# A graph layer on one core: chunks of 896 edges for 768, 58 steps for 68, pieces dealt behind the next sums, another last order, four loads under way for five

## The chip, the core and the metric

The kernel runs on one core of a Trainium2 chip. The metric is device time in microseconds (us) of one execution; lower is better. The core has TensorE (PE; its weight loads are listed as PEld), VectorE (DVE), ScalarE (ACT), GpSimd (POOL) and SyncE (SP, which here only issues DMAs), and 16 DMA engines. SBUF has 128 partitions, PSUM holds what PE writes.

## What is computed

One layer of a graph network, all in float32: 12500 nodes with 128 features, 412500 edges with 48 features, sorted by their target node `dst`. The features of a node's edges are summed; the node's own features are normalised; both go through two dense layers, with a residual.

```python
h = jnp.maximum(_layernorm(x, axis=-1), 0.0)
# in the layer: nodes = h, edges = edge_attr_48
agg = jax.ops.segment_sum(edges, recv, num_segments=N_NODES)   # recv = dst
u = graph_globals[batch]                                       # batch is all 0
z = jnp.concatenate([nodes, agg, u], axis=1)                   # 128 + 48 + 64
h2 = jax.nn.relu(z @ W1 + b1)                                  # 256
x = x + (h2 @ W2 + b2)
```

## The kernel before

**Edges.** The edges are cut into chunks of `CE = 768`: `T = 6` consecutive edges in each of 128 partitions, so that a partition's row is 6 x 48 x 4 = 1152 bytes. There are 537 chunks and 84 edges over. Since the edges are sorted, the targets of one chunk lie within a window of `W = 32` consecutive nodes. Eight chunks (`CS`) make a step, four (`CH`) a half step; 67 whole steps and a last one of one chunk and the rest make `NS = 68`.

For a step, `load` (L259) has SP issue four DMAs of two chunks each. `onehot` (L265) has DVE compare the edges' positions in their windows (`rel`) with 0 to 31; the result is a 128 x 32 matrix of zeros and ones for each of the 48 groups of edges. `aggregate` (L287) has PE multiply them with the edges' features: four chunks use four column groups of 32, and the products of a half step lie side by side in one PSUM bank. `keep_sums` (L301) has ACT copy the sums to SBUF. `place_columns` (L308, DVE) makes a matrix of zeros and ones that says at which node of the step each of the 128 sums belongs, `place` (L314) multiplies with it on PE, and `add` (L323, DVE) adds the outcome, 218 columns wide, into `aggT`, the sums of all nodes, at a column that is read from the data (`at_i`, within 47 of a planned centre, `SLACK`).

**Targets.** `dst` comes in five parts of up to 128 chunks. `load_dst` loads a part with a chunk in each partition, `shift_dst` (L178) subtracts a reference, the chunk's middle edge less 16, `spread_dst` (L229) transposes it on PE into `rel`, in two halves of three edge positions, `own_and_ref` (L190) and `middles` (L201) work out where chunks and steps belong. `check_dst`, `deviation`, `worst_of_all` and `verdict` find whether a target lies outside its window; if one does, a general branch behind `tc.If` (L744) computes everything again.

**Nodes.** 12500 nodes make 26 blocks: one of 212, 23 of 512, and two of 256 at the end, `x1` and `x2`. A block goes through `load_x`, `stats`, `root`, `factors`, `plus_b2`, `normal` (normalisation), `turn` and `keep` (transposed and copied), `first_h` (the x part of the first layer), `first_a` (the part of the sums, once its steps are added), `relu`, `second` (second layer, two rows of 128 nodes a call), `result` and `store`. Stores go by POOL's queue, those of the last two blocks by SP's.

**Order.** Each engine does its instructions in the order in which the program writes them. The loop over steps (L694) writes: placement of an earlier step, loads of the step `AHEAD - 1 = 4` further on, what is dealt to half step `2s`, the add, what is dealt to `2s + 1`, the step's sums, copies, comparisons for two steps further on. From `LATE = NS - 8` on a step is placed one step after its sums instead of two. `piece` (L601) deals PE's pieces of the layers (turn, first_h, first_a, second) to half steps, one after another, by a cost in us and a room per half step: `SHARE = 1.05`, and 1.3 for the last 28 half steps. Loads and normalisation of a block are dealt at fixed distances ahead of its turn (`load_x` 20 half steps, L638).

**Loads under way.** `few` (L254) makes each load of edges (and the later ones of x and dst) wait until the load `FLIGHT = 5` before it has landed. There are 22 buffers for edges (L140), each of two chunks.

**The end** is written by hand (L722 to L738): first layer of x2 (its x part), x1's sum part and relu, placement and add of the last step, x1's second layer, result and store, then the same for x2.

Of the kernel before, what the change touches and what calls it, by code (L numbers as in the profile page):

```python
# [22 lines left out]
def kernel(  # L23
# [25 lines left out]
    T = 6  # L49
# [5 lines left out]
    BEFORE, SECOND, WP = 118, 102, 116  # L55
# [5 lines left out]
    assert NCH == NSF * CS + 1 and TAIL % T == 0 and 0 < TAIL  # L61
    TP = TAIL // T


    PER = 11
# [3 lines left out]
    HALF = (2 * CH + 1) * CE * N // (2 * E)  # L69
    LAST = (2 * NCH - 1) * CE * N // (2 * E)  # L70
    SLACK = 47

    def centre(s):
        return SPAN * (s // PER) + EACH * (s % PER) + HALF if s < NSF else LAST

# [52 lines left out]
    def load_tail(e):  # L128
        nc.sync.dma_start(e[:TP], edge_attr[NCH * CE:E].rearrange("(p t) d -> p (t d)", t=T))

# [8 lines left out]
    with fast:  # L139
        ep = fast.enter_context(tc.tile_pool(name="edges", bufs=22))  # L140
# [11 lines left out]
        NCK = 4 * len(parts) + 2  # L152
# [25 lines left out]
        def shift_dst(i):  # L178
            c0, rows = parts[i]
            di = dsts[i]  # L180
            sub = dp.tile([P, 1], F32, name="sub")
            mid = dp.tile([P, 1], F32, name="mid")
# [4 lines left out]
            dsts[i] = df, mid  # L187


        def own_and_ref(i):  # L190
            n, rows = parts[i][1] // CS, parts[i][1]
            df, mid = dsts[i]
            a = dp.tile([P, P // CH], F32, name="own")
            nc.vector.tensor_scalar(a[:rows, :2 * n], same_h[:rows, :2 * n], mid[:rows], None, OP.mult)
            b = dp.tile([P, P // CS, 2], F32, name="ref")
            nc.vector.tensor_scalar(
                b[:rows, :n], perm[:rows, 0].rearrange("k (s h) -> k s h", h=2)[:, :n, 1:2].to_broadcast([rows, n, 2]),
                mid[:rows], -1.0, OP.mult, OP.mult)
            dsts[i] = df, mid, a, b

        def middles(i):  # L201
# [3 lines left out]
            _, mid, a, b = dsts[i]  # L205
            pt = ps_t.tile([P, 512], F32, name="pt") if i else ps_o.tile([P, 512], F32, name="po")
            nc.tensor.matmul(pt[:, :2 * n], same_c[:rows].rearrange("k c w -> k (c w)"), a[:rows, :2 * n],
# [4 lines left out]
            nc.tensor.matmul(pt[0:1, row:row + n], mid[:rows],  # L212
                             perm[:rows, 0].rearrange("k (s h) -> k s h", h=2)[:, :n, 1], start=False, stop=True,
                             skip_group_check=True)
            m = n
            if i == len(parts) - 1:
                nc.tensor.matmul(pt[0:1, row + n:row + n + 1], mid[:rows], perm[:rows, 0, 2 * n:2 * n + 1],
                                 start=False, stop=True, skip_group_check=True)
                m = n + 1
            nc.vector.tensor_tensor(pos[:, s0:s0 + n], pt[:, :2 * n].rearrange("p (s h) -> p s h", h=2),  # L220
                                    wcol[:, None, :].to_broadcast([P, n, 2]), OP.add)
            r = slice(s0, s0 + m)
            mf = dp.tile([1, P], F32, name="mf")
            nc.vector.tensor_tensor(dev[:, r], pt[0:1, row:row + m], cen[:, r], OP.subtract)
# [4 lines left out]
        def spread_dst(i, h):  # L229
            c0, rows = parts[i]  # L230
            dv = dsts[i][0].rearrange("c (p t) -> c t p", t=T)
            pool, name = ((ps_o, "po"), (ps_h, "ph"))[i] if h and i < 2 else (ps_t, "pt")
            pt = pool.tile([P, 512], F32, name=name)
            for t in range(3):
                nc.tensor.transpose(pt[:, t * rows:(t + 1) * rows], dv[:rows, 3 * h + t, :], ident[:rows, :rows])
            nc.scalar.copy(
                rel[:, c0:c0 + rows, 3 * h:3 * h + 3].rearrange("p c t -> p t c"),
                pt[:, :3 * rows].rearrange("p (t c) -> p t c", t=3))

        def outside(v, n, m, col, most=over):  # L240
            sc = mp.tile([P, CE], F32, name="sc")
# [17 lines left out]
        def load(s, h):  # L259
            for c in range(CH * h, CH * (h + 1), 2) if s < NSF else range(2 * h, 2, 2):  # L260
                e = ep.tile([P, 2, T * DE], F32, name="e")
                few(load_edges(e, s * CS + c, 2 if s < NSF else 1))
                edges.setdefault(s, []).extend([e[:, 0], e[:, 1] if s < NSF else etail])

        def onehot(s):  # L265
# [10 lines left out]
            if s == NSF:  # L276
                chunks(0, 1)
                compare(P, T, 2 * T, relt)
# [7 lines left out]

        def aggregate(s, h):  # L287
            whole = s < NSF
            if h == 0:
                banks_s[s] = ps_agg.tile([P, 512], F32, name="ps")[:, :2 * DE].rearrange("p (h f) -> p h f", h=2)  # L290
                if not whole:
                    return
            ps, es, oh = banks_s[s], edges[s], onehots[s]
            for t in range(T):
                for q in range(CH) if whole else range(2):
                    c = CH * h + q if whole else q
                    nc.tensor.matmul(  # L297
                        ps[W * q:W * (q + 1), h], oh[:, c * T + t], es[c][:, t * DE:(t + 1) * DE],
                        start=(t == 0 and (h == 0 or not whole)), stop=(t == T - 1), skip_group_check=True)

        def keep_sums(s):  # L301
            h = slice(0, 2) if s < NSF else slice(1, 2)
            k = P if s < NSF else 2 * W
            to = sums[s % NSB].rearrange("p h (u f) -> p h u f", u=2)[:k, h, :, :DE]
            ps = banks_s.pop(s)
            nc.scalar.copy(to, ps[:k, h, None, :].to_broadcast([k, h.stop - h.start, 2, DE]))  # L306
# [7 lines left out]
        def place(s):  # L314
            banks_p[s] = pp = ps_p.tile([P, 512], F32, name="pp")
            po = places.pop(s)
            whole = s < NSF
            k = P if whole else 2 * W
            for h in range(2) if whole else (1,):
                nc.tensor.matmul(pp[:HI + DE, SECOND * h:SECOND * h + WP], sums[s % NSB][:k, h, :HI + DE], po[:k, h],  # L320
                                 start=(h == 0 or not whole), stop=(h == 1), skip_group_check=True)

        def add(s):  # L323
# [3 lines left out]
            a = 0 if s < NSF else SECOND  # L327
            to = aggT[:, ds(v[0] + a, WG - a)]
            nc.vector.tensor_tensor(to, to, banks_p.pop(s)[:HI + DE, a:WG], OP.add)  # L329
# [68 lines left out]
        def bank(j, h):  # L398
            n = blocks[j][1] * blocks[j][2]
            small = bank_is_shared(j)  # L400
            if h == 0 or not small:
                pool, name = (ps_t, "pt") if j == NBL - 2 else (ps_h, "ph")
# [77 lines left out]
        tail_di = one.tile([P, T], I32)  # L480
# [3 lines left out]
        def load_tail_dst():  # L484
            ta = NCH * CE
            at = ta - CE // 2
            load_tail(etail)
            with nc.allow_non_contiguous_dma(reason="84 numbers, once"):
                nc.sync.dma_start(tail_di[:TP], dst[ta:E].rearrange("(p t) -> p t", t=T))
                nc.sync.dma_start(tail_md[:TP], dst[None, at:at + 1].to_broadcast([TP, 1]))  # L490

        def tail_dst():
            sub = one.tile([P, 1], F32)
            nc.vector.tensor_scalar(sub[:TP], tail_md[:TP], float(-W // 4), None, OP.add)
            nc.vector.tensor_scalar(relt[:TP], tail_di[:TP], sub[:TP], None, OP.subtract)
            outside(relt[:TP], TP, T, 4 * len(parts))
            nc.vector.tensor_copy(pos[:, NSF], wcol[:, 1:2].to_broadcast([P, 2]))
            nc.vector.tensor_scalar(pos[W:2 * W, NSF], pos[W:2 * W, NSF], float(W // 4), None, OP.add)
# [12 lines left out]
        AHEAD = 5  # L511
        EARLY = 2
        FLIGHT = 5
        LATE = NS - 8
        with tc.manual_schedule():
# [14 lines left out]
            nc.gpsimd.memset(cen[:, NSF:NS], float(LAST))  # L530
# [66 lines left out]
            SHARE, LAST_SHARE = 1.05, 1.3  # L597
# [13 lines left out]

            def turned(j):
# [10 lines left out]
            for j in range(NW):  # L623
# [4 lines left out]
                for q in range(0, r, 2):  # L628
# [3 lines left out]
                at(where["o", j] + 1, result, j)  # L632
                at(where["o", j] + 1, store, j)
            where["turn", NBL - 2], where["turn", NBL - 1] = where["turn", NW - 1] + 2, where["turn", NW - 1] + 4
# [32 lines left out]
            for i in range(2, len(parts)):  # L667
                need = 2 * (parts[i][0] // CS)
# [6 lines left out]
                at(k - 16, load_dst, i)  # L675
            at(2 * (NS - 44), clear_tail)
            at(2 * (NS - 40), load_tail_dst)
            at(2 * (NS - 20), tail_dst)
            at(2 * (NS - 10), deviation)
            at(2 * (NS - 9), worst_of_all)  # L680
            apart(2 * (NS - 7), verdict)
# [8 lines left out]
            for h in range(NH):  # L690
                at(where["turn", x2] + 2, first_h, x1, h)
            assert placed(ready[x1]) < NS

            for s in range(NS):  # L694
# [39 lines left out]
            first_a(x2)  # L734
            relu(x2)
# [8 lines left out]
    with tc.If(isbad >= 1):  # L744
# [3 lines left out]
        with tc.tile_pool(name="any", bufs=1) as ap, tc.tile_pool(  # L748
# [37 lines left out]
            for t in range(T):  # L786
                pt = pp.tile([P, P], F32, name="pt2")
                nc.tensor.transpose(pt[:TP, :1], f1.rearrange("c (p t) -> c t p", t=T)[:, t, :], ident[:1, :1])
# [25 lines left out]
            e = ap.tile([P, T * DE], F32, name="e3")  # L814
            load_tail(e)
# [63 lines left out]
```

## Time and profile before

| what | value |
|---|---|
| three runs | median 328.39 us (326.06 to 328.59) |
| the profiled execution | 327.03 us |
| its span, first to last instruction | 325.0 us |
| mean granted TensorE clock | 0.991 |
| DMA | 95.33 MB, mean 293 GB/s |
| comparisons for sums (L269, DVE) | 70 instructions, 117.5 us, 1682 ns each |
| matmuls of the sums (L297, PE) | 6444 records (two for each matmul), 98.2 us |
| placement (L320, PE) | 270 records, 43.8 us, 285 ns each |
| placement columns (L310, DVE) | 68, 38.9 us, 573 ns each |
| add (L329, DVE) | 68, 25.8 us, 379 ns each |
| copy of sums (L306, ACT) | 68, 21.7 us, 318 ns each |

The span is that of the same profiled execution; the 2 us between it and the time lie outside the traced instructions. "Busy" is the time in which an engine has an instruction running; "idle before" is put down to what ended it. A DMA record is one packet (here one row of a partition) on one of the 16 engines. A row of the timeline gives start, length, engine, line, operation, operands, how many were merged, and in brackets the idle time ahead of it with what ended it; SPq is SP's DMA queue.

### The profile page before, as it was taken

The numbers are of one execution on the slowest core, as the hardware profiler recorded it, in microseconds if no ns is written. First come the engines' busy times: TensorE is split into PE (matmuls) and PEld (weight loads), VectorE is DVE, ScalarE is ACT, GpSimd is POOL, SyncE is SP. The second block draws the span as 40 slices with busy tenths as digits, with TensorE's granted clock in tenths as the row PEclk, the third lists the DMA queues.
The fourth block names the chain that finished last, engine by engine and source line by source line (L and its number), as shares of the span: only waits on it lengthen the run. The fifth ranks groups of instructions, "written<-read, shape, count | busy, mean of one in ns | idle before, by whom it ended". The sixth has DMA issues, their size and how long they took to land. (4 is left out here: it accounts for less than half of the span.)

```text
span 325.0 us, 17324 instructions
## 1 busy us (share of the span) xinstructions
PE 281.6 (87%) x7598; PEld 212.8 (65%) x7599; DVE 236.3 (73%) x560; ACT 138.9 (43%) x325; POOL 67.9 (21%) x88
## 2 busy tenths in 40 slices
PE   7789779889879879999788998699998988899992
PEld 3557566767657666778576766476775776676771
DVE  6867978757689757978578867867777789587621
ACT  2226733445346431636183535053654154336410
POOL 8331212033113203201303301204200402301000
PEclk9999999999999998999999999999999999999998
DMA  7999999999999999999989999999999999899611
GB/s 227 281 321 305 302 312 309 308 309 317 314 304 332 295 331 282 316 340 343 337 255 310 310 322 314 290 307 340 310 330 307 285 332 319 275 324 329 212 36 39
DMA packets 80045, 95.33 MB, mean 293 GB/s; under 512 B 5473, under 2 KB 74851, under 8 KB 79964
## 3 DMA queue, kind: packets, MB, share of 16 engines
q1 hardware_dynamic: 77756, 87.53, 85.9%
q0 software_dynamic: 2208, 6.63, 5.3%
q8 instruction: 61, 1.00, 1.4%
q14 instruction: 20, 0.16, 0.2%
HBM read 87.74 MB, written 6.40 MB: 290 GB/s over the span
## 5 line engine op out<-in xcount | busy, mean ns | idle before, releaser
L297 PE MATMUL ps<-e,oh 128*32 128x48 f32 x6444 | 98.2, 208 | 30.8 <-issue 17.3
L297 PEld LDWEIGHTS ps<-e,oh 128*32 128x32 f32 x6444 | 81.5, 110 | 62.6 <-issue 32.2
L269 DVE TENSOR_TENSOR oh<-iota,rel 128x1536 f32<-128x1536 f32 (+1 forms) x70 | 117.5, 1682 | 0.0
L306 ACT COPY sums<-ps 128x192 f32<-128x192 f32 x68 | 21.7, 318 | 129.2 <-PE ps L297 129.2
L329 DVE TENSOR_TENSOR aggT<-aggT,pp 112x218 f32 x68 | 25.8, 379 | 50.0 <-PE pp L320 43.0
L455 POOL DMA_DIRECT2D out_dram<-ot x25 | 13.9, 556 | 230.3 <-DVE ot L447 75.5
L442 PE MATMUL po<-w,hid 128*128 128x128 f32 (+1 forms) x384 | 49.4, 280 | 1.2 <-issue 0.8
L408 PE MATMUL ph<-hT,w1h 128*128 128x512 f32 (+2 forms) x100 | 48.5, 589 | 0.1
L442 PEld LDWEIGHTS po<-w,hid 128*128 128x128 f32 (+1 forms) x384 | 46.4, 195 | 1.9 <-issue 0.9
L320 PE MATMUL pp<-place,sums 128*112 128x116 f32 x270 | 43.8, 285 | 0.7 <-issue 0.7
L433 ACT ACTIVATE hid<-ph,bias 128x512 f32<-128x512 f32 (+2 forms) x49 | 30.4, 670 | 31.8 <-PE ph L422 31.8
L376 ACT ACTIVATE xn<-xt,sh,sc 128x128 f32<-128x128 f32 (+1 forms) x98 | 40.5, 486 | 0.0
L369 POOL TENSOR_TENSOR xb<-xt,b_sb 128x512 f32<-128x512 f32 (+2 forms) x26 | 35.9, 1384 | 15.4 <-DMA xt<-in_x_dram 9.6
L310 DVE TENSOR_TENSOR place<-iota,pos 128x232 f32<-128x232 f32 x68 | 38.9, 573 | 0.0
L320 PEld LDWEIGHTS pp<-place,sums 128*112 128x112 f32 x270 | 32.2, 177 | 5.6 <-issue 1.7
L390 ACT COPY hT<-pt 128x512 f32<-128x512 f32 (+2 forms) x26 | 26.4, 1015 | 7.0 <-PE pt L384 6.9
L422 PE MATMUL ph<-aggT,w1a 48*128 48x256 f32 (+1 forms) x192 | 27.8, 401 | 0.0
L447 DVE TENSOR_TENSOR ot<-po,xb 128x512 f32<-128x512 f32 (+2 forms) x25 | 16.7, 666 | 11.5 <-PE po L442 7.9
L422 PEld LDWEIGHTS ph<-aggT,w1a 48*128 48x128 f32 x192 | 16.8, 186 | 10.5 <-issue 7.1
L346 DVE BATCH_NORM_STATS2 st<-xt 128x6 f32<-128x128 f32 (+1 forms) x98 | 21.3, 279 | 2.9 <-DMA xt<-in_x_dram 2.9
L408 PEld LDWEIGHTS ph<-hT,w1h 128*128 128x128 f32 x100 | 16.4, 194 | 5.9 <-issue 3.1
L384 PE MATMUL pt<-ident,xn 128*128 128x128 f32 (+1 forms) x98 | 17.4, 285 | 1.4 <-ACT xn L376 0.8
(122 smaller groups left out, 143.0 us busy)
## 6 DMA issues: line engine op xcount, KB each, us to landing
e<-in_edge_attr_dram SPq DMA_DIRECT2D x268, 288.0 KB, 4.7
xt<-in_x_dram SPq DMA_DIRECT2D x23, 256.0 KB, 5.0
out_dram<-ot POOLq DMA_DIRECT2D x23, 256.0 KB, 5.0
di<-in_dst_dram SPq DMA_DIRECT2D x3, 384.0 KB, 5.7
di<-in_dst_dram SPq DMA_DIRECT2D x1, 363.0 KB
xt<-in_x_dram SPq DMA_DIRECT2D x2, 128.0 KB, 4.2
out_dram<-ot SPq DMA_DIRECT2D x2, 128.0 KB
e<-in_edge_attr_dram SPq DMA_DIRECT2D x1, 144.0 KB
```

The costliest lines, as they stand in the source:

```text
L269: nc.vector.tensor_tensor(oh[:k, a:b], iota[:k, None, :W].to_broadcast([k, b - a, W]), r[:, :, None].to_broadcast([k, b - a, W]), OP.is_equal)
L297: nc.tensor.matmul(ps[W * q:W * (q + 1), h], oh[:, c * T + t], es[c][:, t * DE:(t + 1) * DE], start=(t == 0 and (h == 0 or not whole)), st ...
L310: nc.vector.tensor_tensor(po, iota[:, None, :WP].to_broadcast([P, 2, WP]), pos[:, s, :, None].to_broadcast([P, 2, WP]), OP.is_equal)
L320: nc.tensor.matmul(pp[:HI + DE, SECOND * h:SECOND * h + WP], sums[s % NSB][:k, h, :HI + DE], po[:k, h], start=(h == 0 or not whole), stop= ...
L329: nc.vector.tensor_tensor(to, to, banks_p.pop(s)[:HI + DE, a:WG], OP.add)
L369: nc.gpsimd.tensor_tensor(xb[:m, :r], xs[j][:m, :r], b2_sb[:m, None, :].to_broadcast([m, r, D]), OP.add)
L376: nc.scalar.activation(xn[:m, q], xs[j][:m, q], AF.Relu, bias=shift[j][:m, q:q + 1], scale=scale[j][:m, q:q + 1])
L390: nc.scalar.copy(hT[:, :m * r].rearrange("d (p r) -> d r p", r=r), ht[j][:, :m * r].rearrange("d (r p) -> d r p", r=r))
L408: nc.tensor.matmul(ph, w1h[:, h * P:(h + 1) * P], ht[j][:, :n], start=(h == 0 or not small), stop=False, skip_group_check=True)
L422: nc.tensor.matmul(hids[j, h][:, q:q + w], w1a[k, h * P:(h + 1) * P], aggT[k, c:c + w], start=False, stop=True, skip_group_check=True)
L433: nc.scalar.activation(to, ph, AF.Relu, bias=bias[:, h:h + 1])
L442: nc.tensor.matmul(pos_o[j][:m, q], hids[j][:, h, q, :m], w2[:, h], start=(h == 0), stop=(h == NH - 1))
```

## The change

- `T = 7`: a partition's row has seven edges (1344 bytes), a chunk 896, there are 460 chunks and 340 edges over. 57 whole steps and a last one of four chunks and the rest make `NS = 58`. The rest is laid out as four edges (`TT`) in each of 85 partitions.
- A window begins at the chunk's first edge, not 16 below its middle one. Half steps are placed by first edges: the second half's origin is column 118 (`SECOND`, 102 before), the placement is 128 wide (`WP`, 116 before), the add 246 (218).
- `spread_dst` transposes four and three edge positions; the last step's place comes from the rest's first edge (`put_at` in `tail_dst`), after which `deviation`, `worst_of_all` and `verdict` follow two half steps apart. The last part of the targets is dealt four steps earlier than its first chunk asks.
- 18 edge buffers for 22, `AHEAD = 4` for 5, `FLIGHT = 4` for 5; x loads are dealt 17 half steps ahead for 20, dst loads 14 for 16.
- `SHARE`, `LAST_SHARE` are 1.25 and 1.5 (for the last 24 half steps). A block's `first_h` is dealt to the next step behind its `turn`, and `second` to the next step behind `first_a` (`behind`), where it was two half steps further on before.
- `LATE = NS - 7`. The end is written in another order: both small blocks' `first_h`, then placement and add of the last step, half of the second layer of the last 512 block, sum parts and relus of both small blocks, the other half, then their second layers.

```diff
-    T = 6
+    T = 7
...
-    BEFORE, SECOND, WP = 118, 102, 116
+    BEFORE = SECOND = 118
+    WP = P
...
-    assert NCH == NSF * CS + 1 and TAIL % T == 0 and 0 < TAIL
-    TP = TAIL // T
+    assert NCH == NSF * CS + CH and 0 < TAIL
+    TT = next(t for t in range(1, T + 1) if TAIL % t == 0 and TAIL // t <= P)
+    TP = TAIL // TT
...
-        ep = fast.enter_context(tc.tile_pool(name="edges", bufs=22))
+        ep = fast.enter_context(tc.tile_pool(name="edges", bufs=18))
...
-            nc.vector.tensor_scalar(sub[:rows], di[:rows, CE // 2:CE // 2 + 1], float(-W // 2), None, OP.add)
+            nc.vector.tensor_copy(first[:rows], di[:rows, 0:1])
...
-            nc.vector.tensor_scalar(df[:rows], di[:rows], sub[:rows], None, OP.subtract)
-            nc.vector.tensor_scalar(mid[:rows], sub[:rows], float(W // 2), None, OP.add)
+            nc.vector.tensor_scalar(df[:rows], di[:rows], first[:rows], None, OP.subtract)
...
+            put_at(slice(s0, s0 + n), pt[0:1, row:row + n])
+
+        def put_at(r, nodes):
+            m = r.stop - r.start
             mf = dp.tile([1, P], F32, name="mf")
-            nc.vector.tensor_tensor(dev[:, r], pt[0:1, row:row + m], cen[:, r], OP.subtract)
+            nc.vector.tensor_tensor(dev[:, r], nodes, cen[:, r], OP.subtract)
...
-        AHEAD = 5
+        AHEAD = 4
         EARLY = 2
-        FLIGHT = 5
-        LATE = NS - 8
+        FLIGHT = 4
+        LATE = NS - 7
...
-            SHARE, LAST_SHARE = 1.05, 1.3
+            SHARE, LAST_SHARE = 1.25, 1.5
...
-                while room.setdefault(k, (SHARE if k < 2 * NS - 28 else LAST_SHARE) + min(0.5, room.get(k - 1, 0.0))) < us / 2:
+                while room.setdefault(k, (SHARE if k < 2 * NS - 24 else LAST_SHARE) + min(0.5, room.get(k - 1, 0.0))) < us / 2:
...
+            def behind(name, j):
+                return where[name, j] // 2 * 2 + 2
...
-                piece("h0", j, where["turn", j] + 2, us, (first_h, (j, 0)))
+                piece("h0", j, behind("turn", j), us, (first_h, (j, 0)))
...
-                    piece("o", j, where["a", j] + 2, 0.9, (second, (j, q)))
+                    piece("o", j, behind("a", j), 0.9, (second, (j, q)))
...
-                    at(k - 20, load_x, j)
+                    at(k - 17, load_x, j)
...
-                need = 2 * (parts[i][0] // CS)
+                need = 2 * (parts[i][0] // CS - (4 if i == len(parts) - 1 else 0))
...
-                at(k - 16, load_dst, i)
+                at(k - 14, load_dst, i)
...
+            first_h(x1, 0)
+            first_h(x1, 1)
             first_h(x2, 0)
             first_h(x2, 1)
+            place(NS - 1)
+            add(NS - 1)
             for k in sorted(todo):
                 for f, a in todo.pop(k):
                     f(*a)
+            second(NW - 1, 0)
             first_a(x1)
             relu(x1)
-            place(NS - 1)
-            add(NS - 1)
+            first_a(x2)
+            relu(x2)
+            second(NW - 1, 2)
+            result(NW - 1)
+            store(NW - 1)
             second(x1, 0)
             result(x1)
             store(x1)
-            first_a(x2)
-            relu(x2)
             second(x2, 0)
             result(x2)
             store(x2)
```

More of the change, by code (lines that the diff above doesn't have):

```diff
@@ L259, in load @@
         def load(s, h):
-            for c in range(CH * h, CH * (h + 1), 2) if s < NSF else range(2 * h, 2, 2):
+            if s == NSF and h:
+                edges[s].append(etail)
+                return
+            for c in range(CH * h, CH * (h + 1), 2):
                 e = ep.tile([P, 2, T * DE], F32, name="e")
-                few(load_edges(e, s * CS + c, 2 if s < NSF else 1))
-                edges.setdefault(s, []).extend([e[:, 0], e[:, 1] if s < NSF else etail])
+                few(load_edges(e, s * CS + c, 2))
+                edges.setdefault(s, []).extend([e[:, 0], e[:, 1]])
         def onehot(s):
@@ L316, in place @@
             po = places.pop(s)
-            whole = s < NSF
-            k = P if whole else 2 * W
-            for h in range(2) if whole else (1,):
+            for h in range(2):
+                k = W if s == NSF and h else P
                 nc.tensor.matmul(pp[:HI + DE, SECOND * h:SECOND * h + WP], sums[s % NSB][:k, h, :HI + DE], po[:k, h],
-                                 start=(h == 0 or not whole), stop=(h == 1), skip_group_check=True)
+                                 start=(h == 0), stop=(h == 1), skip_group_check=True)
         def add(s):
@@ L485, in load_tail_dst @@
             ta = NCH * CE
-            at = ta - CE // 2
             load_tail(etail)
-            with nc.allow_non_contiguous_dma(reason="84 numbers, once"):
-                nc.sync.dma_start(tail_di[:TP], dst[ta:E].rearrange("(p t) -> p t", t=T))
-                nc.sync.dma_start(tail_md[:TP], dst[None, at:at + 1].to_broadcast([TP, 1]))
+            with nc.allow_non_contiguous_dma(reason="some hundred numbers, once"):
+                nc.sync.dma_start(tail_di[:TP], dst[ta:E].rearrange("(p t) -> p t", t=TT))
+                nc.sync.dma_start(tail_md, dst[None, ta:ta + 1].to_broadcast([P, 1]))
         def tail_dst():
[L493 to L498, printed above, removed]
+            first = one.tile([P, 1], F32)
+            nc.vector.tensor_copy(first, tail_md)
+            nc.vector.tensor_scalar(relt[:TP, :TT], tail_di[:TP], first[:TP], None, OP.subtract)
+            outside(relt[:TP, :TT], TP, TT, 4 * len(parts))
+            nc.vector.tensor_scalar(pos[:, NSF, 0:1], pos[:, NSF, 0:1], first, None, OP.subtract)
+            nc.vector.tensor_copy(pos[:, NSF, 1:2], wcol[:, 1:2])
+            outside(pos[:, NSF], P, 2, 4 * len(parts) + 2, overp)
+            put_at(slice(NSF, NS), first[0:1])
         worst = one.tile([P, 1], F32)
@@ L627 @@
                     turned(j + 1)
-                for q in range(0, r, 2):
-                    piece("o", j, where["a", j] + 2, 0.9, (second, (j, q)))
+                for q in range(0, r, 2) if j + 1 < NW else ():
+                    piece("o", j, behind("a", j), 0.9, (second, (j, q)))
                 if j + 1 < NW:
                     hidden_x(j + 1)
-                at(where["o", j] + 1, result, j)
-                at(where["o", j] + 1, store, j)
-            where["turn", NBL - 2], where["turn", NBL - 1] = where["turn", NW - 1] + 2, where["turn", NW - 1] + 4
+                    at(where["o", j] + 1, result, j)
+                    at(where["o", j] + 1, store, j)
+            for j in (NBL - 2, NBL - 1):
+                where["turn", j] = behind("turn", j - 1)
+            assert where["a", NW - 1] < 2 * NS and where["turn", NBL - 1] < 2 * NS
             for j in range(NBL):
@@ L814 @@
             e = ap.tile([P, T * DE], F32, name="e3")
+            nc.vector.memset(e, 0.0)
             load_tail(e)
```

103 lines of the change are left out of this document (47 added, 56 removed).

## The prediction

> **What bounds the kernel now.** I read the page's DMA rows first, then the DMA queue's own waits, then the table by stages, and last the timeline of the end.
>
> ```profile
> span 325.0 us, 17324 instructions
> DMA  7999999999999999999989999999999999899611
> GB/s 227 281 321 305 302 312 309 308 309 317 314 304 332 295 331 282 316 340 343 337 255 310 310 322 314 290 307 340 310 330 307 285 332 319 275 324 329 212 36 39
> q1 hardware_dynamic: 77756, 87.53, 85.9%
> ...
> e<-in_edge_attr_dram SPq DMA_DIRECT2D x268, 288.0 KB, 4.7
> ```
>
> The 16 DMA engines are busy from the second slice to the 37th (about 8 to 300 us), at some 310 GB/s. Of what they move, the edge loads are 79.2 of 95.3 MB. A load lands 4.7 us after its issue.
>
> ```profile
> SPq L125 <- DMA e<-in_edge_attr_dram: 116.2, 210, 2.6
> SPq L125 <- PE ps L297: 17.3, 37, 2.1
> PEld ps L297 <- DMA e<-in_edge_attr_dram: 17.2, 28, 1.5
> PE ps L297 <- DMA e<-in_edge_attr_dram: 12.8, 22, 1.4
> ```
>
> SP spends 116 us waiting for an earlier edge load to land: the cap of five loads under way. The second row names PE's buffer releases; but counting issued tiles (two chunks each) against tiles consumed gives 4 to 8.5 outstanding of 22 buffers, so PE had long released them and the wait is again the landing. PE itself stands still for edges (last two rows). So up to about 305 us the DMA stream is the clock.
>
> ```profile
> 256.00:288.00 32.00, 28.28 (x813) 21.11 (x800) 25.34 (x64) 13.94 (x31) 8.18 (x9) 1.00 0.98 312
> ...
> 300.00:304.00 4.00, 4.00 (x113) 3.05 (x112) 2.57 (x4) 2.00 (x6) 0.00 (x0) 1.00 1.02 333
> 304.00:308.00 4.00, 4.00 (x122) 3.10 (x124) 1.62 (x5) 1.44 (x4) 0.56 (x1) 1.00 0.45 159
> 308.00:312.00 4.00, 4.00 (x119) 3.83 (x119) 0.69 (x2) 1.15 (x3) 0.00 (x0) 1.00 0.02 4
> ```
>
> Columns: window, its length, PE, PEld, DVE, ACT, POOL busy, clock, DMA share, GB/s. At 304 to 308 the DMA share falls to 0.45 (the last edge packet ends at 305.7); from 300 on PE has no idle time left: the end is PE's.
>
> ```profile
> 315.72 0.30 PEld L442 LDWEIGHTS po<-w,hid 128*128 128x128 f32 x2 [0.55 <-ACT hid L433]
> ...
> 318.42 0.97 PEld L442 LDWEIGHTS pp<-w,hid 128*128 128x128 f32 x8 [1.02 <-ACT hid L433]
> ...
> 319.68 0.42 DVE L447 TENSOR_TENSOR ot<-pp,xb 128x256 f32<-128x256 f32 x1 [1.31 <-PEq L744]
> ```
>
> In the last chain PE also stands still, for 0.55 and 1.02 us here, because a block's second product follows its own relu directly. The last result is done at 320.1; its store and the closing take 4.9 us.
>
> So the span is stream (305.7) plus end (19.3). The profiled execution took 327.03, its span 325.0, so 2.0 lie around it; the median of the three runs is 328.39, 0.4% above. The sum is made against 327.03.
>
> **The change, part by part.**
>
> *Larger packets.* The trace's packet records, grouped by size, have medians of 51 ns for 1152 B (68750 of them: the edge rows of one chunk in a partition), 84 for 2048, 121 for 3072, 159 for 4096. That is linear: about 37 ns for 1 KB and 9 fixed. Records of one engine overlap: matched end to start, the starts are 47 ns apart for 1152 B and 80 for 2048, so 36.8 ns for 1 KiB more at the same slope, and 4.6 fixed; a 1344 B row comes to 54.1 ns. Before: 68750 x 47 / 16 = 202.0 us per engine. After: 460 x 128 = 58880 rows x 54.1 / 16 = 199.1. **-2.9**. The loads go from 269 to 230 (and the tail's own), so 16 x 39 4-byte completion records less, 5 ns apart: **-0.2**.
>
> *Stalled packets.* The mean 1152 B record is 58.5 ns, 7.5 over its median: 32 us per engine, in single packets of 100 to 1400 ns. The cause is not in the trace. Were it one price per packet, 58880 packets would save 4.6; per byte, nothing. The 2048 B loads have a mean of 95.2, 11.2 over: 1.5 times for 1.78 times the bytes. So nearly per byte; I take **-1.0** (ends -4.6 and 0).
>
> *Four loads under way for five.* 5 x 294912 = 1.475 MB become 4 x 344064 = 1.376 MB, 6.7% less. At an issue the loads not yet started hold on average 2.2 loads of work (bytes issued less bytes started), at 0.79 us each 1.76 us; from issue to the first packet goes 0.85 us (first store of the end: issued 317.72, packets from 318.5). Slack 0.9 us. Afterwards 3 x 0.905 us stand ahead, less the same 1.4 that an average engine is past the load that lands: 1.35, slack 0.5. The engines' gaps sum to 24 us, 0.08 us per issue where 2 to 2.75 loads stand ahead, 0.13 at 1.5 to 1.75, 0.15 at 1.25 to 1.5. A half load less for some 255 issues makes 0 to +10; I take **+2.5**, the nearer quarter, since issues with a short queue in this trace stand behind a stalled packet, which idles the others under any cap.
>
> *Steps 68 to 58.* Work per edge is the same: 3222 by 3224 matmuls, and comparisons of 1792 for 1536 elements. Per step there is less: placement (0.5 us of PE; now 128 for 116 columns, some 0.53), add, column comparison, copy of sums. DVE: 58 x (1.96 + 0.63 + 0.43) = 175 for 182 us; PE: 58 x 1.88 for 68 x 1.66 = 109 for 113 us. Until 305 all this lies beside the stream (PE 28.3, DVE 25.3 of 32 us): nothing. If that cover is gone, PE's 109 and the layers' unchanged 150 are still below 300.
>
> *x, dst, tail and checks.* An x load is dealt 17 half steps ahead for 20; a half step grows from 2.25 to 2.6 us, and SP's edge loads stand 3 steps ahead for 4. With the 1 to 2 steps that SP is ahead of PE, it leads its statistics by some 13 us either way, against a landing of 5.0. Destinations (14 for 16) the same. If late, DVE waits as it did twice (2.9 us in all), and behind it the comparisons. The shift by a chunk's first edge drops one small DVE operation a part; the last part adds about ten small DVE and ACT operations (0.15 to 0.6 us) six to nine steps before the end. 18 buffers for at most 9 tiles outstanding: no wait. POOL only sees its stores regrouped. Nothing. The widest chunk of the inputs spans 30 nodes of 32, so the general branch stays untaken.
>
> *The end.* Priced by rows of the end: 48 pairs of sums 1.16 us (56: 1.35), placement 0.5, first layer of a 512 block 1.9 and 1.06, turn 0.66 or 0.3, second layer 0.95 for two rows. Edges of a step arrive every 4 x 0.97 us before, every 4 x 1.1 after. Walking PE's written order from nine steps back, taking at each step the later of data and PE, the last sums start 4.9 us after the last edge packet in the old order (measured 6.6) and 1.8 in the new: a step gives PE more time for a piece, and only half a step has to come last. Behind them the new order has 8.4 us of PE (sums 0.8, two first layers 1.9, placement 0.5, eight rows of second layer 3.8, two aggregate parts 1.2, the last drain 0.2) with no relu directly ahead of its product; the old one took 7.3 with its waits. Result 0.4 and closing 4.9 as before. 1.8 + 8.4 + 0.4 + 4.9 = 15.5 against 17.5 by the same walk: -2.0, or -3.8 against the measured 19.3. I take **-2.5** (0 to -5).
>
> *Sum:* -2.9 - 0.2 - 1.0 + 2.5 - 2.5 = -4.1: **322.9**, 1.7% below the median.
>
> **Rivals.**
>
> 1. *Four loads starve the stream partly*: +7 to +10 instead of +2.5. For it: idle per issue rises as the queue shortens. Against: 85% of the idle time comes with full queues. About 328.5, no change.
>
> 2. *Starts off a 256-byte boundary.* 1152 B rows start on it or 128 off and touch five 256-byte pieces; 1344 B rows start 0, 64, 128 or 192 off and touch six. If an engine pays by pieces (2048 to 3072 B: 37 ns for four, 9.3 each), a row costs 56.3 for 54.1: 8.1 us, so 331. Against: 1152 B at five pieces should take 56 ns, and both kinds of start read 51 (the lower three quarters all do). [...]
>
> 3. *Slower: the cap becomes the clock.* Bytes under way over landing time is the rate: 1.475 MB / 4.7 us = 314 GB/s. With 1.376 MB the landing must fall to 4.39 us to hold it. It decides from about 4.5: the stream then loses 2.5%, 7 us. Stuck at 4.7, the 270 us that such loads fill become 288: about 341. For it: SP already waits on landings nearly throughout. Against: the shortest landing is 3.3, so the rest is queueing, which four loads shorten.
>
> 4. *More is won:* stalls per packet and the end at -5: near 317.
>
> **How the numbers follow.** Forecast, 318 to 327: 0.58. Rival 1: 0.17. Rival 2: 0.06. Rival 3: 0.10 (332 and above). Rival 4: 0.09. A measurement of this kernel tells about 1%: faster is below 325.1, slower above 331.7. Faster: 0.52 of the forecast and rival 4, 0.61. Same: 0.06 of the forecast, 0.16 of rival 1, 0.05 of rival 2, 0.27. Slower: the rest, 0.12. The range goes to rival 4 below and rivals 1 and 2 above: 317 to 330.
>
> **What would show it.** 58880 records of 1344 B with a median near 58 (60 or more: rival 2). Landing of e at 4.3 to 4.4 (4.5 or more: rivals 1 and 3) and mean rate in the stream at or above 310 GB/s. Last edge packet near 304. Last sums starting within 4 us behind it, and no PE wait of half a microsecond on ACT after them; last result some 10.6 us behind the last edge packet. Wrong if the stream ends later than 306, or if x or dst loads appear among DVE's waits.

## The result, and the profile after

The changed kernel takes **337.68 us** (median of 6 runs, 335.1 to 340.5) against 327.23 for the kernel before (6 runs, 324.22 to 329.46): a ratio of 1.0336, 95% interval 1.0246 to 1.0427. It is slower, and lies above the predicted range. Ratios, here and below, leave out the runs that a slower state of the chip lengthened. The profiled execution took 336.89 us, its span 334.8, against 327.03 and 325.0: 9.8 us more.

The page of the changed kernel, in the order in which the kernel before was read:

```profile
span 334.8 us, 17081 instructions
...
DMA  7999999999999999999999999999999998989702
GB/s 237 271 319 300 288 279 288 342 292 318 292 303 290 289 305 298 319 312 309 289 312 326 291 320 291 276 322 313 282 312 332 286 309 260 290 289 311 251 2 70
...
q1 hardware_dynamic: 67439, 87.53, 82.7%
...
e<-in_edge_attr_dram SPq DMA_DIRECT2D x230, 336.0 KB, 4.7
```

The load is larger (336 for 288 KB), there are fewer of them, and each still lands **4.7 us** after its issue. The rates in the slices are nearer to 300 than to 310 GB/s. The steady part in one row each, first the kernel before, then the changed one (window, length, PE, PEld, DVE, ACT, POOL busy, clock, DMA share, GB/s):

```profile
32.00:288.00 256.00, 225.18 (x6356) 172.73 (x6343) 194.95 (x447) 117.27 (x274) 50.90 (x58) 0.99 0.98 312
```

```profile
304.00:308.00 4.00, 4.00 (x126) 2.74 (x126) 3.45 (x4) 0.32 (x1) 1.30 (x2) 1.00 1.02 340
...
312.00:316.00 4.00, 4.00 (x73) 2.90 (x75) 1.15 (x3) 0.82 (x3) 0.56 (x1) 1.00 0.91 306
316.00:320.00 4.00, 3.99 (x159) 3.22 (x145) 1.03 (x3) 1.88 (x4) 0.00 (x0) 1.00 0.05 17
...
32.00:288.00 256.00, 217.80 (x6161) 166.34 (x6148) 191.83 (x418) 116.92 (x266) 55.88 (x56) 1.00 0.94 302
```

312 GB/s became 302, and the share of busy DMA time fell from 0.98 to 0.94. The DMA falls silent at 316 to 320, not at 304 to 308: the last edge packet ends at 316.7 (305.7 before). So the stream lost 11.0 us, and what comes behind it shrank by 1.2 (18.1 us for 19.3). The waits say who stood still:

```profile
SPq L127 <- DMA e<-in_edge_attr_dram: 150.0, 192, 4.6
```

```profile
PEld ps L301 <- DMA e<-in_edge_attr_dram: 42.4, 62, 1.9
```

SP waits 150 us for earlier edge loads to land (116 before), and PE's weight loads stand 42.4 us for edges (17.2 before). The end, from the last sums on:

```profile
318.63 1.02 PE L301 MATMUL ps<-e,oh 128*32 128x48 f32 x56
...
327.42 0.97 PEld L443 LDWEIGHTS po<-w,hid 128*128 128x128 f32 x8 [1.43 <-ACTq L755]
327.44 1.13 PE L443 MATMUL po<-w,hid 128*128 128x128 f32 x8 [1.27 <-DVE ot L448]
...
329.56 0.42 DVE L448 TENSOR_TENSOR ot<-pp,xb 128x256 f32<-128x256 f32 x1 [0.47 <-PEq L755]
```

The last sums start 1.9 us behind the last edge packet (predicted: 1.8). No product waits for its own relu any more, but x1's second layer waits 1.27 us for DVE to read the PSUM bank `po` of the last 512 block: a new wait. The last result is done at 330.0, 13.2 us behind the last edge packet (predicted: 10.6).

### The profile page after: what moved, and what is told of

Same layout as the page of the kernel before. It is cut to its first block, busy times and chain, and to the rows that moved or that the text cites. A ratio compares the mean times of both kernels' runs of the same rounds, so it can differ in the third digit from the quotient of the medians.

```text
span 334.8 us, 17081 instructions
## 1 busy us (share of the span) xinstructions
PE 281.5 (84%) x7555; PEld 212.8 (64%) x7556; DVE 235.5 (70%) x530; ACT 139.5 (42%) x320; POOL 72.3 (22%) x87
## 5 line engine op out<-in xcount | busy, mean ns | idle before, releaser
L301 PE MATMUL ps<-e,oh 128*32 128x48 f32 x6440 | 102.9, 210 | 42.1 <-DMA e<-in_edge_attr_dram 32.9
L301 PEld LDWEIGHTS ps<-e,oh 128*32 128x32 f32 x6440 | 84.3, 112 | 73.7 <-DMA e<-in_edge_attr_dram 42.4
L276 DVE TENSOR_TENSOR oh<-iota,rel 128x1792 f32<-128x1792 f32 (+1 forms) x60 | 115.9, 1935 | 0.0
L309 ACT COPY sums<-ps 128x192 f32<-128x192 f32 (+2 forms) x59 | 18.7, 318 | 131.2 <-PE ps L301 131.2
L330 DVE TENSOR_TENSOR aggT<-aggT,pp 112x246 f32 x58 | 23.7, 409 | 56.2 <-PE pp L322 47.4
L443 PE MATMUL po<-w,hid 128*128 128x128 f32 (+1 forms) x384 | 47.7, 277 | 1.3 <-DVE ot L448 1.3
L370 POOL TENSOR_TENSOR xb<-xt,b_sb 128x512 f32<-128x512 f32 (+2 forms) x26 | 40.5, 1558 | 17.2 <-DMA xt<-in_x_dram 10.8
L322 PE MATMUL pp<-place,sums 128*112 128x128 f32 x232 | 39.8, 295 | 0.0
L313 DVE TENSOR_TENSOR place<-iota,pos 128x256 f32<-128x256 f32 x58 | 37.6, 649 | 0.0
L322 PEld LDWEIGHTS pp<-place,sums 128*112 128x112 f32 x232 | 29.2, 178 | 5.1 <-issue 1.5
```

What stands on the lines that cost most here:

```text
L276: nc.vector.tensor_tensor(oh[:k, a:b], iota[:k, None, :W].to_broadcast([k, b - a, W]), r[:, :, None].to_broadcast([k, b - a, W]), OP.is_equal)
L301: nc.tensor.matmul(ps[W * q:W * (q + 1), h], oh[:, c * T + t], es[c][:, t * DE:(t + 1) * DE], start=(t == 0 and h == 0), stop=(t == (TT if ...
L313: nc.vector.tensor_tensor(po, iota[:, None, :WP].to_broadcast([P, 2, WP]), pos[:, s, :, None].to_broadcast([P, 2, WP]), OP.is_equal)
L330: nc.vector.tensor_tensor(to, to, banks_p.pop(s)[:HI + DE, :WG], OP.add)
L370: nc.gpsimd.tensor_tensor(xb[:m, :r], xs[j][:m, :r], b2_sb[:m, None, :].to_broadcast([m, r, D]), OP.add)
L443: nc.tensor.matmul(pos_o[j][:m, q], hids[j][:, h, q, :m], w2[:, h], start=(h == 0), stop=(h == NH - 1))
```

## The experiments

The theories on record: **C**, the cap sets the rate (bytes under way over landing time, rival 3); **R**, the longer rows or fewer packets are dear in themselves; **P**, PE's work slows the loads, by its reads of SBUF (**S**) or by fetching its instructions (**F**: the packets of 16384 bytes on the queue that the page calls instruction, 61 in the kernel before, 60 in the changed one; it also says that PE's waits called issue are waits for such fetches); **Q**, PE's own pace is the limit once edges come early enough; **D**, the dealing of the pieces holds PE. Each ratio is against the kernel before on the same chip. "Stream end" is the end of the last edge packet of the profiled execution. Kernels from the changed one are called a_, from the one before b_. The granted clock of the profiled executions was 0.95 to 0.99, but 0.87 in a_thin, 0.93 in b_thin and 0.88 in b_thin1, from which only the stream is read (the stream did not follow that clock in b_thin1: at 0.88 it ends at 306.3, in the kernel before, at 0.99, at 305.7).

### The cap alone, in the changed kernel

```diff
-        FLIGHT = 4
+        FLIGHT = 5        # a_flight5; 6 in a_flight6
```

> The changed kernel with five loads under way instead of four, nothing else (5 x 344064 B = 1.72 MB under way). Theory C (the cap of four is what slowed it): landing rises to about 5.2 us, the rate of the stream is back above 315 GB/s, the last edge packet ends near 303 and the time is 322 to 326. Theory R (rows of 1344 B are served worse, whatever the cap): the mean edge record stays near 68 ns over a median of 58, the time stays within 1.5% of 337.

> The changed kernel with six loads under way (2.06 MB). Theory C: the gaps of the DMA engines shrink further, 318 to 324 us, less gained than from four to five. Theory R: no faster than with five, near 337.

Five loads: 332.39 us, ratio 1.0256 (1.0172 to 1.034). Six: 327.74, ratio 1.0142 (1.0045 to 1.0238). Their streams end at **299.5** and **294.5** for 316.7, so one load more under way gave back 17.2 us of stream, more than was lost. That is C's stream (near 303) and C's landing (5.2). Its times were 322 to 326 and 318 to 324, and both were missed: the time hardly follows. With five loads the ratio's interval overlaps that of the changed kernel (1.0256 against 1.0336), so in time that gain is not clear of the noise; by time alone 332.39 would fit R. a_flight5, waits and windows:

```profile
PEld ps L301 <- issue: 48.8, 51, 3.1
...
PE ps L301 <- issue: 36.5, 35, 3.0
```

```profile
300.00:304.00 4.00, 3.96 (x127) 2.68 (x125) 3.42 (x5) 0.32 (x1) 1.30 (x2) 1.00 0.19 70
...
312.00:316.00 4.00, 4.00 (x110) 3.28 (x99) 0.75 (x2) 2.23 (x6) 0.00 (x0) 1.00 0.02 5
```

The DMA is nearly idle from 300 on while PE still works for 25 us: PE is behind. It no longer waits for edges but for "issue", nothing that the profile names: 48.8 us for 18.4 in the changed kernel. With six, SP waits for PE to give buffers free (at the median issue 17 of the 18 buffers are out, counted as in the prediction; 6 in the changed kernel):

```profile
SPq L127 <- PE ps L301: 85.3, 68, 5.1
SPq L127 <- DMA e<-in_edge_attr_dram: 49.7, 87, 2.2
```

C holds for the stream. That the time does not follow fits Q, and F as well: both say that PE is the clock now.

### The cap alone, in the kernel before

```diff
-        FLIGHT = 5
+        FLIGHT = 4        # b_flight4; 6 in b_flight6, 7 in b_flight7
```

> The kernel before with four loads under way instead of five (4 x 294912 B = 1.18 MB). Theory C: bytes under way fall by 20%, the landing time falls by less than that, the stream loses 5% or more: 342 us or above, slower than the changed kernel. Theory R: the cap matters little with 1152 B rows, 327 to 332 us.

> The kernel before with six loads under way (1.77 MB). Theory C alone: no slower than with five (stream ends below 305). Theory C with F (more bytes ahead of each fetch, PE stalls longer, PE becomes the bound): PE's waits called issue rise above 32 us, tail above 24, time 327 to 335, between five (325) and seven (337).

> The kernel before with seven loads under way (2.06 MB). Theory C: gaps of the DMA engines shrink from about 26 us, the time falls by 5 to 20 us, to 308 to 322. Theory R, or five being enough: within 1% of 327.

Four loads of 288 KB: **361.9 us, ratio 1.1165** (1.1059 to 1.127), stream end 343.7. Six: 330.16, ratio 1.0107 (1.0003 to 1.0211), stream end 296.0. Seven: 337.14, ratio 1.0303 (1.0175 to 1.0432), of which only the time is read. Four fits C (342 or above); six fits C with F (327 to 335, with 49.5 us of "issue" before the sums' weight loads and 31.4 us behind the last edge packet); seven fits neither of its forecasts (308 to 322, or within 1% of 327). Of b_flight4:

```profile
e<-in_edge_attr_dram SPq DMA_DIRECT2D x268, 288.0 KB, 4.5
```

```profile
32.00:288.00 256.00, 214.16 (x5628) 163.83 (x5627) 170.90 (x390) 104.59 (x245) 42.97 (x51) 0.95 0.90 277
```

A fifth fewer bytes under way shorten the landing only from 4.7 to 4.5 us, so the rate falls from 312 to 277 GB/s. This landing is a coarse measure: it is the median of the half or so of the loads whose landing the trace gives, and at the same 1.47 MB it reads 4.7, 4.9 and 5.1 us in three runs (before, b_order, b_thin1) whose streams all end at 306. Side by side, the stream ends of both row lengths fall in the order of the bytes under way:

| MB under way | kernel | landing us | stream end us |
|---|---|---|---|
| 1.18 | b_flight4 | 4.5 | 343.7 |
| 1.38 | changed | 4.7 | 316.7 |
| 1.47 | before | 4.7 | 305.7 |
| 1.72 | a_flight5 | 5.2 | 299.5 |
| 1.77 | b_flight6 | 5.2 | 296.0 |
| 2.06 | a_flight6 | 5.4 | 294.5 |

R falls: rows of 1344 bytes are not dearer than those of 1152 (54 and 47 ns from start to start of their records, 0.040 and 0.041 ns a byte). The last rows flatten; with six loads the buffers run out behind PE, as the waits of a_flight6 show (85.3 us). And b_flight6 and b_flight7 did not bring the old kernel anything: its stream ends 9.7 us sooner with six, and it is not faster.

### Loads cut in half

The same rows, nine loads of one chunk under way (1.55 MB) in place of four of two chunks.

```diff
-        for h in range(...): few(load_edges(e, s*CS + CH*h..., 2))
+        for c in range(CH * h, CH * (h + 1)): few(load_edges(e, s * CS + c, 1))   # 36 buffers, FLIGHT = 9
```

> The changed kernel with one chunk a load (172032 B) and nine under way, 1.55 MB: between four (1.38) and five (1.72) of the double loads, in finer steps. Theory C with bytes under way as the measure: stream ends between 299 and 316, near 307, time 330 to 335. If completions in finer steps keep the engines fuller than bytes say, the stream ends at 300 or earlier and PE sets the end: 326 to 331.

341.16 us, ratio 1.0465 (1.0401 to 1.0528), stream end 318.0: both forecasts are missed. It is inconclusive on C, because the cap was mostly not reached: at 300 GB/s and a landing of 4.3 us some 1.3 MB are under way in all, not 1.55, and SP waits little for landings:

```profile
SPq L127 <- PE ps L301: 28.7, 71, 1.3
SPq L127 <- DMA e<-in_edge_attr_dram: 18.9, 34, 1.7
```

18.9 us in place of 150, or 47.6 if the first row too is a landing (at most 20 of the 36 buffers are out, so PE had released the one asked for). SP's issues now sum to 243 us, 0.49 us each on average (113 us in the changed kernel): SP's issuing, likely, took the cap's place.

### Is the landing only the queue's? Sums left out

a_thin and b_thin leave out the sums of all but one of the seven (six) edge positions; every load is still made. Each was run twice.

```diff
-                for t in range(T):
+                for t in range(1):
```

> The changed kernel (four loads under way) with the sums cut to one of the seven edge positions: the other six are left out, so the node sums are incomplete. All loads stay. PE loses some 75 us of work and most of its instruction fetches. If the cap alone sets the stream (theory C), the last edge packet still ends near 316 us and landing stays at 4.7. If PE's work, its reads or its fetches slow the loads (theory P), the stream ends below 308.

> The kernel before (five loads under way) with the sums cut to one of six edge positions, the rest left out. Theory C: the last edge packet still ends near 305, 10 us ahead of the changed kernel's. Theory P: both thin kernels end their streams within 4 us of each other, and below 300.

a_thin: 320.18 us, ratio 0.9829 (0.9756 to 0.9903), stream end **302.7** (316.7), at the same cap of four. b_thin: 301.2 and 309.9 us, stream end **284.4** (305.7), at the same cap of five. By C alone with a fixed landing neither should have moved; a_thin's loads land in 4.4 us for 4.7, b_thin's in 4.5 for 4.7. By P alone both streams should have ended within 4 us of each other; they are 18.3 apart. So the cap and something in PE's work both set the rate. What else went: of b_thin's page and windows,

```profile
span 299.2 us, 6564 instructions
...
q8 instruction: 19, 0.31, 0.4%
```

```profile
32.00:288.00 256.00, 215.15 (x2017) 151.76 (x2017) 210.45 (x473) 124.88 (x291) 54.58 (x62) 0.93 1.01 331
```

331 GB/s in place of 312, with 6564 instructions in place of 17324 and 19 packets on the instruction queue for 61. To part reads from instructions, b_thin1 issues all matmuls again, but with one of the 48 features at five of the six positions (those sums are left out):

```diff
+                    w = DE if t == 0 else 1
-                    nc.tensor.matmul(ps[..., h, :], ..., es[c][:, t * DE:(t + 1) * DE])
+                    nc.tensor.matmul(ps[..., h, :w], ..., es[c][:, t * DE:t * DE + w])
```

> The kernel before with one feature of 48 summed at five of the six edge positions (the other 47 are left out there): every matmul and weight load is issued, so PE's instructions and the 61 packets that fetch them are back, but PE reads little of the edges. Theory F (fetches on single DMA engines hold up the loads under way): the last edge packet ends at 300 to 306, as in the full kernel, against 284.4 without these instructions. Theory S (PE's reads of the edges in SBUF slow the loads, or PE's work does): it ends within 5 us of 284.

```profile
span 333.0 us, 17324 instructions
...
q8 instruction: 61, 1.00, 1.3%
```

```profile
32.00:288.00 256.00, 227.69 (x6247) 180.89 (x6241) 192.13 (x434) 117.22 (x274) 48.44 (x55) 0.89 0.99 313
```

Stream end **306.3**, as in the kernel before, with 53 of 288 edge columns read by the matmuls. (Its time, 333.79 us and a ratio of 1.0238, has PE's end at a clock of 0.88 in it and is not read.) S falls for the reads of edges, and what comes back with the instructions is 21.9 us. If the 42 packets of 16384 bytes that came back were all of it, each would cost 0.52 us of stream.

A single run can be asked the same, where the packets are far enough apart: 13 to 22 us in the two thin kernels. In b_thin, between 20 us and the stream's last 6 us, the other packets move 322 GB/s in the 5 us from the start of such a packet and 339 in the rest, a loss of 0.25 us for each; in a_thin 292 and 323, a loss of 0.48. Packets laid at random places in these traces give as much in 3% and 0.2% of the cases. So F is borne out inside the runs, by these figures at about half of the 0.52 where the cap is five. What makes the other half is not shown: the weight loads, and the matmuls with their short reads, came back with the instructions as well. The packet, one record, occupies one DMA engine for some 1.1 us (median 1.09 us in the kernel before, 1.00 in the changed one), while a load has rows on all 16: each of the 339 transfers of the kernel before leaves 16 records of 4 bytes, 5428 in all.

### PE without the stream

a_still loads the edges of the first four steps alone and sums those again in every later step; PE's instructions are all there.

```diff
     def load(s):
+        if s >= 4:
+            edges[s] = edges[s % 4][:4] + [etail] if s == NSF else edges[s % 4]
+            return
```

> The changed kernel that loads the edges of the first four steps only and sums them again in all later steps: 93% of the edge traffic is left out, PE has all its work. Shows PE's own floor. Theory F (PE's waits that the profile calls issue are instruction fetches that stand behind edge loads): these waits fall from 26 us (both PE rows of the sums) to under 8, and the time is 285 to 300. If such waits come from PE's own pace (theory Q), they stay at 20 us or more.

282.96 us, ratio 0.8687 (0.861 to 0.8763). Page, and waits:

```profile
span 282.4 us, 16623 instructions
...
q8 instruction: 60, 0.98, 1.5%
...
out_dram<-ot POOLq DMA_DIRECT2D x23, 256.0 KB, 2.6
```

```profile
PEld ps L304 <- issue: 10.7, 19, 1.5
```

With 7% of the edge traffic the span is 282.4 us. With the same work for PE, a stream that is over by 294.5 and edges in plenty, it is 324.6 (a_flight6). The waits called issue come to 11.4 us (both PE rows), nearer to F's "under 8" than to Q's "20 or more", and neither; the time is a little below F's range. The same row in the kernel before, and in the changed kernel:

```profile
PEld ps L297 <- issue: 32.2, 41, 2.1
```

```profile
PEld ps L301 <- issue: 18.4, 26, 1.5
```

"Issue" before sums is 10.7 us in a_still, where PE waits 3.9 us for edges, and 48.8 in a_flight5, where it waits 2.0: that is what the traffic adds. That it is only 18.4 in the changed kernel, beside 42.4 us of waits for edges, may be because these waits cover the pauses; some 44 to 50 in a_flight5, a_flight6 and b_flight6 are then what stands there without the cover. One such pause in a_flight6, in PE's timeline:

```profile
208.39 1.31 PE L301 MATMUL ps<-e,oh 128*32 128x48 f32 x103
212.65 0.32 PE L301 MATMUL ps<-e,oh 128*32 128x48 f32 x9 [2.96 <-issue]
```

PE stops for 2.96 us in the middle of a half step whose edges are there; a packet of 16384 bytes on the instruction queue runs from 210.16 to 211.32. Of PE's pauses of over 0.7 us that are put down to issue, 30.1 us in that run, those in which such a packet ends make 19.7 us; packets laid at random would give about 10. In b_flight6 it is 21.4 of 30.2, in a_flight5 21.8 of 34.0, both against some 11. That these pauses are PE waiting for instructions is inferred from that and from their shrinking with the traffic; no run removed the fetches and kept all else.

### The order of the pieces and of the end

b_order is the kernel before (rows of 1152 bytes, five loads) with the new dealing, `LATE` and last order. a_f6_early is a_flight6 with more room per half step.

```diff
-            SHARE, LAST_SHARE = 1.25, 1.5
+            SHARE, LAST_SHARE = 1.6, 2.0        # a_f6_early
```

> The kernel before (768 edges a chunk, five loads under way) with the new dealing (behind, 1.25 and 1.5, LATE) and the new last order only. If these are the gain that the prediction's last term says: stream end unchanged at 305 to 306, tail 16 to 18 for 19.4, time 1 to 3 us less than before. If the new dealing pushes PE's work to the end, the tail is 20 or more and the time 1% higher.

> The changed kernel with six loads under way and wider shares (1.6 and 2.0 for 1.25 and 1.5), so that pieces are dealt earlier. With six loads the stream ends near 294 us and 30 us of PE work follow. If PE is simply the bound there (theory F: its waits are instruction fetches, which no order of the pieces fills), the time stays within 1% of 327.7 and the tail near 30. If the dealing holds PE's work back to the end (theory D), the tail falls below 25 and the time below 323, under the kernel before.

b_order: 329.33 us, ratio 1.0132 (1.0042 to 1.0222); its profiled execution has a stream end of 306.0 and a span of 324.5, against 305.7 and 325.0. So in the trace the end is 0.8 us shorter (18.5 us, between its two forecasts), and the timed runs are 1.3% longer; what the other runs lose is not in that trace and stays open. The new order is no gain that these runs can show. a_f6_early: 329.32, ratio 1.0131 (1.0022 to 1.024), 30.6 us behind its last edge packet, with 45.7 us of "issue" before the sums' weight loads for 43.9: D falls, dealing earlier does not take PE's pauses away.

No version that makes all the sums beat the kernel before. Rows of 1344 bytes with the old dealing were not tried: by `piece`'s own costs they do not fit into 58 steps at the old `SHARE`. So how much of the ratios of a_flight5 and a_flight6 is the new dealing's is open.

## Why the prediction was wrong

- **The step that failed is "Four loads under way for five"**, taken at +2.5 with ends of 0 and +10. The stream ended 11.0 us later where the sum of the stream's terms was -1.6, and giving the fifth load back alone moved it by 17.2. The error lies in the landing: the prediction counted on 4.3 to 4.4 us, because it took the 1.4 us by which 4.7 exceeds the shortest landing (3.3) as queueing that four loads shorten. Measured, the landing stayed at 4.7, and in the kernel before four loads of 288 KB land in 4.5 us for 4.7 with five. The landing hardly gets shorter with fewer bytes, so bytes under way set the rate. That is the mechanism of rival 3, given 0.10; its "stuck at 4.7" is what the trace shows. Its 341 still has the +2.5 of this term in it; without that the same sum is 338.4, against 337.7 measured. Rival 1 had the direction and the wrong size, +7 to +10 and 328.5.
- **The slack was reckoned from averages** (0.9 us before, 0.5 after). What they leave out are late rows on single engines: the longest record of a row of 1344 bytes is 1.56 us, the median 58 ns. SP's next issue waits until a load has landed whole (150 us of such waits), so that, by the author's estimate, one engine held for 1.1 us by an instruction packet can leave the other 15 without work. The lower rates behind such packets fit this (322 for 339 GB/s in b_thin, 292 for 323 in a_thin); that it is what empties the engines here is argued and not shown. The idle time of the engines between 20 us and the stream's last 6 us, summed from the packet records, is some 24 us per engine before, 33 after and 50 in b_flight4. The row that spoke for it was there, SP waiting on landings nearly throughout; the prediction named it and gave it one chance in ten.
- **"Larger packets"** was right in the price of a row: 58880 records of 1344 bytes, median 58.0 ns, starts 54 ns apart as forecast, and at a cap of five the stream ends 6.2 us earlier than before (the three packet terms made -4.1, but 1.72 MB under way help as well, so the two are not parted).
- **"Stalled packets" was not won**: the records' excess over their median is 36.7 us per engine for 32.4 before. In a_flight5 it is 26.1, in b_flight4 41.5: it goes with the cap, not with the size.
- **Rival 2 is out.** Its sign was a median of 60 ns or more; from the 5th to the 75th percentile the records of 1344 bytes read 58 ns, so the four kinds of start, a quarter of the rows each, do not part, and this trace shows no cost of a start off the boundary. That an engine pays by pieces of 256 bytes was the author's assumption; no run shows it.
- **"Steps 68 to 58 ... nothing" held only while the stream was late.** The cover named was PE's 259 us of sums, placement and layers below 300. Between them stand the pauses put down to "issue": 32.2 us before the sums' weight loads in the kernel before, a row that the prediction does not show beside the 17.2 for edges, and for which it has no term. With six loads the span is 324.6 though the edges are all in by 294.5, so even a stream that ended 22 us earlier did not reach the forecast's span of 320.9.
- **"The end", -2.5**, came to -1.2 in the profiled execution. The last sums came as walked, 1.9 us behind the last packet, but PE then took 10.8 us for 8.4: among it, x1's second layer waits 1.27 us for a PSUM bank, which the walk did not model (it took PE and data alone, not the bank's reader), and the sums take 1.3 us for 0.8.
- **x, dst, tail and checks**: DVE waits 3.1 us for x (2.9 before) and 3.5 for dst (2.6), all before 30 us. Right, as far as these waits show.

## What to carry to other kernels

The cap on transfers under way was part of the rate here: 1.18 MB under way moved 277 GB/s, 1.47 MB 312, at landings of 4.5 and 4.7 us. So divide bytes under way by the landing time, and assume that the landing stays where it is until a run shows it shorter; and price the longest waits that no other row explains, as "issue" here. Where the landings in a trace barely reach the next issue, a larger transfer that is paid for with fewer of them can cost more than it gives, as here: 6.7% fewer bytes under way, and a stream that ended 11.0 us later. Before pricing a faster stream, look for the second clock just behind it: here PE, with edges in plenty, paused more and gave a span of 324.6 us, no shorter than the 325.0 of the kernel before.

## What the runs showed of the hardware

Packets of 16384 bytes on the instruction queue (60 in the changed kernel, some 1.1 us each on one DMA engine) cost the stream some 0.25 us apiece in b_thin and 0.48 in a_thin, by the rate behind them; the difference between b_thin and b_thin1 would make 0.52. Their number goes with the instructions: 61 where a page counts 17324, in the kernel before and in b_thin1, 19 where it counts 6564, in b_thin. If PE's pauses are waits for them, one took 2.96 us beside the loads (in the middle of a half step of a_flight6, above), and in a_still, with 7% of the edge traffic, the longest ahead of sums took 1.5 us. About half of a landing under full traffic is that traffic: POOL's stores of 256 KB land after 2.6 us in a_still and 5.0 in the kernel before. And more loads under way were not better: in the kernel before six took 1.0107 and seven 1.0303 times as long as five.
